# Softmax maxima of an attention kernel folded through DRAM, and its SP transfers issued a few to a turn

## The chip, the cores and the metric

The kernel runs on one core of a Trainium2 chip. The metric is device time in microseconds, the median of 3 runs: 1323.48 us before the change (1323.15 to 1324.08). In the text, PE is the matrix engine, ACT the scalar engine (activations), DVE the vector engine, POOL the general engine, and SP the engine that here only issues transfers.

## What is computed

One transformer block in float32 on x of shape (4, 1024, 256): attention with 16 heads of 16, then a gated feed-forward block of width 1024. Both are "sandwiched": layer norm goes in, layer norm comes out, and the result is added to x.

```python
def stable_softmax(x):
    x_max = jnp.max(x, axis=-1, keepdims=True)
    exp_x = jnp.exp(jnp.clip(x - x_max, -50.0, 50.0))
    return exp_x / (jnp.sum(exp_x, axis=-1, keepdims=True) + 1e-6)
...
scores = einsum('bhqd,bhkd->bhqk', q, k) * scale
out = einsum('bhqk,bhkd->bhqd', stable_softmax(scores), v)
...
x = x + layernorm(attention(layernorm(x)))
x = x + layernorm(ffn(layernorm(x)))   # silu(w1)*w2, gelu(h1), gelu(h2), w3
```

The kernel takes the exponential of the scores without subtracting their maximum. The small 1e-6 beside the sum then has to be multiplied by the largest exponential of the row: denominator = 1e-6 * max + sum. The kernel keeps that maximum only for the first 128 queries of each half of a sequence; it is what the change is about.

## The kernel before

**Attention, in tiles.** A *tile* is one (batch b, group g of 4 heads, half h of 512 queries, chunk c of 128 keys, pair u of heads): 4 x 4 x 2 x 8 x 2 = 512 tiles, in this order. For each, `exponentials` (L444) lets PE make scores `s` of 128 keys x 2 heads x 512 queries into one of three two-bank slots of PSUM (pool `ps`, tag `big`), and ACT writes their exponentials `e` into a ring of four pairs of tiles. `weigh` (L454) multiplies a pair of tiles by the values `vaug` into the one-bank accumulator `acc`; a column of ones in `vaug` gives the sum beside the 16 outputs of each head, so each head has a slot of 32 rows of which 17 are used. `rise` (L461) folds a pair into the running maximum `top` on DVE, 128 keys x 4 heads x 128 queries.

**Units.** 16 tiles with one (b, g, h) are a *unit*; there are 32, and two units (both halves) are a group's work. At its end `unit_end` (L632) copies `acc` to `o` on DVE and adds the division (`divide`, L470) to the side work: PE transposes the four heads of `top` (L478) and the four blocks of `o` (L480) into a slot of tag `big`, DVE reduces the transposed maxima to `em` (L482), makes denominators and their reciprocals, and writes the quotients to `on` (L488). After a batch's last group the `ending` follows: transposes of `on`, output projection, norm, residual.

**Turns and side work.** The main loop (L937) works in *turns*: three tiles of scores and exponentials, the maxima and weighted sums of earlier tiles, then one call of `side.take` (L582). Everything else (projections for the next batch, flags, endings, divisions, copies of weights to a rounded form) consists of `Step`s in chains. A turn takes at most one step with PE work; a step is due `gap` turns after the one before it in its chain. In a *calm* turn, close to a unit's end, only PE steps are taken. Steps marked heavy are not taken in two turns running. PE steps other than divisions use the one-bank space `misc`, the *side bank*. A division sets `side.borrowed`, and the next turn then makes one tile fewer before its weighted sums.

**Transfers.** The order in which each engine gets its instructions is the order of the program. SP issues, among others, the *stacks*: for a group, q and k, split into high and low parts, are copied from `cq`/`ck` into 64-row layouts `sq`/`sk` by 32 transfers of 64 KB (`copies` L404, `stack` L419). There are two sets of stacks, so the copies for group g + 2 are issued when group g has ended (L661), and wait for its last scores. At the start, `load_rest` (L198) issues the loads of the output weights, x of batches 2 and 3, and scales behind the first stack. Late in the last batch, the feed-forward's weights are loaded into space that q, k and the stacks leave free (L652, L665).

**Feed-forward.** After the last unit, PE multiplies for 8 halves of sequences through the four layers (`gated`, `gelu_layer`, `finish`); side work there is norms and checks of the weights.

Of the kernel before, what the change touches and what calls it, by code (L numbers as in the profile page):

```python
# [18 lines left out]
P = 128  # L19
HEADS = 16  # L20
DH = 16
# [3 lines left out]
PARTS = 4  # L25
ROWS = PARTS * DH
RING = 8
TURN = 3
LN_EPS = 1e-5
SM_EPS = 1e-6  # L30
# [40 lines left out]
class Step:  # L71


    def __init__(self, run, gap=0, tensor=True, heavy=False):
        self.run, self.gap, self.tensor, self.heavy = run, gap, tensor, heavy
        self.ready, self.patient = lambda: True, heavy


# [37 lines left out]
def tile_fast(ctx: ExitStack, tc: tile.TileContext, x, wqk, wv, wo, w1, w1s, w2, w2s, h1, h1s, h2, h2s, w3, w3s, out, bad):  # L116
# [11 lines left out]
    xpool = ctx.enter_context(tc.tile_pool(name="x", bufs=1))  # L128
    small = ctx.enter_context(tc.tile_pool(name="small", bufs=3))
    dram = ctx.enter_context(tc.tile_pool(name="rounded", bufs=1, space=bass.MemoryType.DRAM))  # L130


    xs = [xpool.tile([P, NT, D], F32, tag=f"x{b}", name=f"x{b}") for b in range(B)]
# [8 lines left out]
    def load_x(b, halves=range(NH)):  # L142
        view = x[b].rearrange("(t p) d -> p t d", p=P)
        for h in halves:
            for at, tokens in pieces(h, view):
                nc.sync.dma_start(out=xs[b][:, at, :], in_=tokens)
# [31 lines left out]
    with ExitStack() as actx, ExitStack() as rctx:  # L178
# [11 lines left out]
                    load_x(0, [1])  # L190
        nc.scalar.dma_start(out=wv_sb, in_=wv.rearrange("(c p) d -> p c d", p=P))

        def load_wo(c):
            for h in range(HPT):
                r = SLOT * (HPT * c + h)
                nc.sync.dma_start(out=wo_sb[DH * h : DH * (h + 1), c, :], in_=wo[r : r + DH, :])

        def load_rest():  # L198

            for c in range(DC):  # L200
                load_wo(c)
            for b in range(2, B):
                load_x(b)
            for name, w in (("w1", w1s), ("w2", w2s), ("h1", h1s), ("h2", h2s)):
                nc.sync.dma_start(out=scales[name], in_=w)
            nc.sync.dma_start(out=w3s_sb, in_=w3s.partition_broadcast(P))


        cq = {(w, m, k): keep.tile([P, S], F32R, name=f"c{'qk'[w]}{m}{k}") for w in range(2) for m in range(DC) for k in ("hi", "lo")}
# [25 lines left out]
        def misc(name):  # L235
            return ps_misc.tile([P, NQ], F32, tag="misc", name=name)
# [30 lines left out]
        def prologue(b, space, copy):  # L267
# [60 lines left out]

            def squares(w, m, h):
                def run():  # L330
                    sq = st["sq", w, m] = work.tile([P, NQ], BF16, tag="sq", name="sq", bufs=4)
                    hi = cq[w, m, "hi"][:, h * NQ : (h + 1) * NQ].bitcast(F32)
                    nc.scalar.activation(sq, hi, AF.Square)

                return run
# [68 lines left out]
        def copies(g, w, c0=0, c1=S):  # L404
# [11 lines left out]

            return [copy(u, j, n) for u in range(2) for j in range(PARTS) for n in range(2)]

        def stack(b, g):  # L419
            for w in (1, 0):  # L420
                for copy in copies(g, w):
                    copy(nc.sync)
            stacked[g % 2] = b, g

        def slots(b, g, t0=0, t1=NT):

# [7 lines left out]
            return run  # L434


        stacked, slotted = [None] * 2, [None] * 2
        tiles = [(b, g, h, c, u) for b in range(B) for g in range(NG) for h in range(NH) for c in range(NT) for u in range(2)]

        def pair(k):  # L440
# [20 lines left out]
        def rise(k):  # L461
# [4 lines left out]
            if c:  # L466
                top = tops[b, g, h]
                nc.vector.tensor_max(top, top if c > 1 else pair(k - 2)[:, :, :, 0:P], pair(k)[:, :, :, 0:P])  # L468

        def divide(g, h, o, top):  # L470


            def run():
                side.borrowed = True
                both = ps.tile([P, 2, NQ], F32, tag="big", name="po")
                po, pm = both[:, 0], both[:, 1].rearrange("p (i k) -> p i k", k=P)
                for i in range(HPG):
                    nc.tensor.transpose(pm[:, i], top[:, i // 2, i % 2], ident)  # L478
                for t in range(TPQ):
                    nc.tensor.transpose(po[:, t * P : (t + 1) * P], o[:, t * P : (t + 1) * P], ident)  # L480
                em = small.tile([P, HPG], F32, tag="em", name="em")
                nc.vector.tensor_reduce(em, pm, AX.X, ALU.max)  # L482
                po = po.rearrange("p (t i s) -> p t i s", t=TPQ, s=SLOT)
                den = small.tile([P, TPQ, HPG], F32, tag="den", name="den")
                nc.vector.scalar_tensor_tensor(den[:, 0], em, SM_EPS, po[:, 0, :, DH], ALU.mult, ALU.add)
                nc.vector.tensor_copy(den[:, 1:], po[:, 1:, :, DH])
                nc.vector.reciprocal(den, den)
                nc.vector.tensor_mul(  # L488
                    on[h][:, :, HPG * DH * g : HPG * DH * (g + 1)].rearrange("p t (i e) -> p t i e", e=DH),
                    po[:, :, :, 0:DH], den.unsqueeze(3).to_broadcast([P, TPQ, HPG, DH]),  # L490
                )

            return [Step(run, 1)]

# [56 lines left out]
        class Side:  # L551


            def __init__(self):
                self.first, self.rest, self.slot = [], [], 0
                self.tired = False
                self.borrowed = False

            def add(self, steps, first=False):
                chain = [list(steps), self.slot]  # L560
# [21 lines left out]
            def take(self, calm=False):  # L582

                self.slot += 1
                self.borrowed = False
                free, heavy = True, False
                for chain in self.first + self.rest:
                    while (step := self.due(chain, self.slot, free)) and (step.tensor or not calm):
                        chain[0].pop(0)
                        chain[1] = self.slot  # L590
                        step.run()
                        free = free and not step.tensor
                        heavy = heavy or step.heavy
                self.tired = heavy
# [5 lines left out]
        side = Side()  # L600
        accs, tops, ends, later = {}, {}, {}, {"qk1": None}

        def begin(b):

            if b + 1 < B:
                norm, xt, qk, v, flags = prologue(b + 1, misc, to_vector)

                def first_made():
                    later["qk"] = b + 1
                    side.add(flags[0])  # L610

                def second_made():
                    later["qk1"] = b + 1
                    side.add(flags[1])


                steps = norm[0] + norm[1] + xt[0]
                for i, step in enumerate(qk[0][0]):
                    steps += [step, xt[1][i]]
                steps += xt[1][TPQ // 2 :] + qk[0][1]  # L620

                xt[0][TPQ // 2].ready = lambda: later["qk1"] == later["v"] == b
                v = v + [Step(lambda: later.update(v=b + 1), 0, False)]
                qk1 = sum(qk[1], [])
                for step in qk1:
                    step.gap, step.patient = 2, False
                qk1 = qk1 + [Step(second_made, 0, False)]
                later["rest"] = [Step(lambda: side.add([Step(lambda: None, 5, False)] + qk1), 0, False)] + v

                later["chain"] = side.add([Step(lambda: None, 0 if b else 4, False)] + steps + [Step(first_made, 0, False)])  # L630

        def unit_end(b, g, h):  # L632
# [2 lines left out]
            to_vector(o, accs[b, g, h])  # L635

            assert g or not b or not any(step.tensor for step in ends[b - 1, h][0])
            unit = side.add(divide(g, h, o, tops[b, g, h]), True)
            if g == NG - 1:
                last = ending(b, h, to_scalar if (b, h) == (B - 1, NH - 1) else to_vector)  # L640
                for step in last:
# [7 lines left out]
            if n >= NG:  # L649
                n, at = n - NG, b + 1  # L650
            if b == B - 1 and g == NG - 2:
                load_weights("h1", range(HC // 2))  # L652
            if at < B:
                put = Step(slots(at, n), 0, False)
                if at > b:
                    assert later["qk"] == at
                    later["chain"][0].append(put)
                else:
                    assert later["qk1"] == at
                    put.run()  # L660
                stack(at, n)  # L661
            if g == NG - 3 and b + 1 < B:
                later["chain"][0].extend(later["rest"])
            elif g == NG - 3:
                side.add([Step(lambda n=n: load_weights(n), 1, False) for n in ("w1", "w2", "w3")])  # L665
                side.add([Step(lambda: None, 7, False)] + prepare(0, to_vector))
            if g == NG - 1:
                begin(b + 1)
# [38 lines left out]
        def prepare(n, copy):  # L707
# [24 lines left out]

                return run

            return norm_steps(rows, st) + [Step(apply(i), 1, False) for i in range(0, TPQ, 2)] + [Step(transposes(c), 1) for c in range(DC)]

        def product(p, n, m, i, c):
            for k, half in enumerate(i):
# [180 lines left out]
        v[0].run()  # L919
        alone = False  # L920
        load_x(1)
        stack(0, 1)
        load_rest()
        early = [v[1], Step(slots(0, 0, 0, NT // 2), 0, False)]
        side.add(early + v[2:] + [Step(slots(0, 0), 0, False), Step(slots(0, 1), 0, False)] + sum(qk[1], []) + [Step(lambda: later.update(qk1=0, v=0), 0, False), Step(lambda: side.add(flags[0] + flags[1]), 0, False)])
        begin(0)
        side.add([s for k in blocks for s in round_weights(*k)])
        made = seen = weighed = 0

# [7 lines left out]
        while weighed < len(tiles):  # L937
            n = end = made
            end += TURN
            make(end - side.borrowed)  # L940
            if made == len(tiles):
                n = made
            for k in range(seen, n - 1, 2):
# [260 lines left out]
```

## Time and profile before

| what | value |
|---|---|
| median of 3 runs | 1323.48 us |
| profiled execution: device time, span | 1322.63 us, 1320.8 us |
| granted PE clock | 0.995 |
| busy share of the span: PE, DVE, ACT, POOL | 96%, 53%, 55%, 9% |
| exponentials, 512 of 128 x 1024 | 485.1 us busy, 1034 ns each |
| running maxima of 128 x 512, 192 later ones of a unit | 134.6 us busy, 701 ns each |
| stack copies, 64 KB each, SP | 2.3 us from issue to landing (median) |
| weight loads of 512 KB, POOL | 5.5 us to landing (median) |

The page's strip of 40 slices shows two halves. In the first 20 slices ACT is 70 to 80% busy and the DMA engines 30 to 80%; from slice 21 on ACT falls to 10 to 40% and PE's weight loads rise from 30 to 80%: that is the feed-forward. A busy share averages over both, so each half is read by itself. Rows of matrix work overlap, and their ends are modelled: how far apart their *starts* are tells more of PE than their durations.

### The profile page before, as it was taken

How to read it: one execution, taken by the hardware profiler on the slowest of the kernel's cores; microseconds unless marked ns; L12 is line 12 of the kernel's file. 1: busy time of each engine (PE TensorE's matmuls, PEld its weight loads, DVE VectorE, ACT ScalarE, POOL GpSimd, SP SyncE). 2: the span in 40 equal slices, each digit the busy share in tenths (PEclk: the TensorE clock that was granted, in tenths of full speed). 3: DMA queues.
4: the chain of work that ended last, by engine and by line, in shares of the span. 5: the costliest groups of instructions: out<-in, count | busy, mean ns of one | idle time of the engine just before them, and what ended most of it. 6: DMA issues, size and time to landing. Idle time of an engine off the chain costs nothing.

```text
span 1320.8 us, 21125 instructions
## 1 busy us (share of the span) xinstructions
PE 1267.2 (96%) x8194; PEld 777.2 (59%) x8194; DVE 696.2 (53%) x1518; ACT 724.1 (55%) x902; POOL 119.1 (9%) x166
## 2 busy tenths in 40 slices
PE   7999999999999999988999999999999999999995
PEld 3333333333333333333578888788887888878885
DVE  3456457654685445645662634736446364463533
ACT  4788887888888888898631412314223142231410
POOL 6212112121120000000000000000000000000000
PEclk9999999999999999999999999999999999999998
DMA  4685543466443333343220000201101011020000
GB/s 131 171 212 131 118 114 94 110 143 152 73 114 61 50 50 65 65 95 129 80 113 1 24 1 1 64 25 32 56 1 64 24 33 57 1 64 8 17 0 19
DMA packets 45518, 91.30 MB, mean 69 GB/s; under 512 B 12000, under 2 KB 22880, under 8 KB 45408
## 3 DMA queue, kind: packets, MB, share of 16 engines
q1 hardware_dynamic: 37520, 65.20, 21.4%
q0 software_dynamic: 7360, 24.12, 5.8%
q8 instruction: 67, 1.10, 0.4%
q10 hardware_dynamic: 528, 0.52, 0.1%
q14 instruction: 43, 0.35, 0.1%
HBM read 40.52 MB, written 15.73 MB: 43 GB/s over the span
## 4 chain that ended last, share of the span: by engine, by line
PE 76%; DVE 10%; ACT 9%; issue 3%; POOL 1%; DMA 1%; SPq 0%; ACTq 0%; POOLq 0%; DVEq 0%
PE ph L739 35%; PE acc L459 12%; PE s L451 8%; ACT e L452 7%; PE pg L739 5%; PE pz L792 4%; PE p L259 4%; PE py L259 2%; PE pv L259 2%; DVE top L468 2%; PE po L480 1%; DVE sg L755 1%; DVE o L265 1%; DVE st L94 1%; DVE ha_lo L744 1%
## 5 line engine op out<-in xcount | busy, mean ns | idle before, releaser
L452 ACT ACTIVATE e<-s 128x1024 f32<-128x1024 f32 x512 | 485.1, 1034 | 54.5 <-PE s L451 42.9
L459 PE MATMUL acc<-e,vaug 128*32 128x512 f32 x2048 | 255.1, 600 | 2.6 <-POOL vaug L429 2.6
L775 ACT ACTIVATE a<-ph,h_scale 128x512 f32<-128x512 f32 x128 | 81.1, 686 | 306.6 <-PE ph L739 306.6
L451 PE MATMUL s<-sq,sk 64*128 64x512 f32 x1024 | 193.2, 449 | 17.6 <-ACT e L452 15.0
L739 PE MATMUL ph<-hb_hi,h 128*128 128x512 f32 x512 | 199.5, 390 | 0.0
L739 PE MATMUL ph<-hb_lo,h 128*128 128x512 f32 x512 | 199.4, 389 | 0.0
L451 PEld LDWEIGHTS s<-sq,sk 64*128 64x128 f32 x1024 | 86.2, 184 | 158.3 <-ACT e L452 125.8
L468 DVE TENSOR_TENSOR top<-top,e 128x512 f32<-128x512 f32 x192 | 134.6, 701 | 42.0 <-ACT e L452 35.4
L459 PEld LDWEIGHTS acc<-e,vaug 128*32 128x32 f32 x2048 | 49.2, 108 | 107.2 <-issue 97.6
L104 POOL TENSOR_TENSOR rstd<-ve,minus_half 128x4 f32<-128x4 f32 (+1 forms) x33 | 37.5, 1137 | 803.1 <-DVE ve L102 803.1
L739 PEld LDWEIGHTS ph<-hb_hi,h 128*128 128x128 f32 x512 | 96.1, 188 | 20.2
L739 PEld LDWEIGHTS ph<-hb_lo,h 128*128 128x128 f32 x512 | 96.1, 188 | 20.1
L776 DVE CAST ha_hi<-a 128x512 fp32r<-128x512 f32 x64 | 27.1, 424 | 142.5 <-ACT a L775 142.5
L739 PE MATMUL ph<-ha_hi,sq 128*128 128x512 f32 x256 | 101.8, 398 | 0.3
L739 PE MATMUL ph<-ha_lo,sq 128*128 128x512 f32 x256 | 99.9, 390 | 0.0
L739 PE MATMUL ph<-ha_lo,sk 128*128 128x512 f32 x256 | 99.7, 390 | 0.0
L739 PE MATMUL ph<-ha_hi,sk 128*128 128x512 f32 x256 | 99.7, 390 | 0.0
L753 ACT ACTIVATE sg<-pg,w_scale 128x512 f32<-128x512 f32 x64 | 43.3, 688 | 55.0 <-DVE ha_lo L744 43.1
L755 DVE SCALAR_TENSOR_TENSOR sg<-pg,w_scale,sg 128x512 f32<-128x512 f32 x64 | 47.1, 745 | 48.0 <-ACT sg L753 48.0
L776 DVE CAST hb_hi<-a 128x512 fp32r<-128x512 f32 x64 | 27.0, 422 | 71.3 <-ACT a L775 71.3
L259 PE MATMUL p<-xT,wqk_sb 128*32 128x512 f32 x512 | 61.1, 598 | 1.5 <-ACT xT L262 0.9
L739 PEld LDWEIGHTS ph<-ha_hi,sq 128*128 128x128 f32 x256 | 48.4, 189 | 12.7 <-DVE sg L755 3.3
(158 smaller groups left out, 1648.2 us busy)
## 6 DMA issues: line engine op xcount, KB each, us to landing
w<-in_h_dram POOLq DMA_DIRECT2D x16, 512.0 KB, 5.5
h_r<-wr POOLq DMA_DIRECT2D x16, 512.0 KB, 3.8
x<-in_h_dram SPq DMA_DIRECT2D x32, 256.0 KB, 2.7
sk<-ck1hi SPq DMA_DIRECT2D x64, 64.0 KB, 2.3
sk<-ck1lo SPq DMA_DIRECT2D x64, 64.0 KB, 2.3
sq<-cq1hi SPq DMA_DIRECT2D x64, 64.0 KB, 2.3
sq<-cq1lo SPq DMA_DIRECT2D x64, 64.0 KB, 2.3
h<-h_r SPq DMA_DIRECT2D x8, 512.0 KB, 6.5
```

Source lines behind the costliest of these rows:

```text
L104: nc.gpsimd.tensor_tensor(rstd[:, :n], ve[:, :n], self.minus_half[:, :n], ALU.pow)
L259: nc.tensor.matmul(o[j : j + SLOT, :], w[:, j : j + SLOT], i, **flags)
L451: nc.tensor.matmul(s[:, a, :], stacks[1, g % 2, u][r, c * P : (c + 1) * P], stacks[0, g % 2, u][r, h * NQ : (h + 1) * NQ], start=True, sto ...
L452: nc.scalar.activation(pair(k)[:, u], s, AF.Exp)
L459: nc.tensor.matmul(acc[SLOT * i : SLOT * (i + 1), :], vaug[g % 2][:, c, i, :], pair(k)[:, i // 2, i % 2, :], start=c == 0, stop=c == NT - 1)
L468: nc.vector.tensor_max(top, top if c > 1 else pair(k - 2)[:, :, :, 0:P], pair(k)[:, :, :, 0:P])
L739: nc.tensor.matmul(p, homes[n][c][:, m * P : (m + 1) * P], half[:, c, :], start=c == 0 and k == 0, stop=c == len(homes[n]) - 1 and k == 1)
L753: nc.scalar.activation(sg, p[:, 0, :], AF.Silu, scale=scales["w1"][:, m : m + 1])
L755: nc.vector.scalar_tensor_tensor(sg, p[:, 1, :], scales["w2"][:, m : m + 1], sg, ALU.mult, ALU.mult)
L775: nc.scalar.activation(a, p[:, j, :], AF.Gelu, scale=scales[n][:, m : m + 1])
L776: nc.vector.tensor_copy(o[0][:, m, :], a)
L792: nc.tensor.matmul(p[t], half[:, c, t * P : (t + 1) * P], homes["w3"][c], start=c == 0 and k == 0, stop=c == HC - 1 and k == 1)
```

## The change

The maxima of a unit no longer go through four transposes. `top` (128 keys x 4 heads x 128 queries) is written to DRAM at the unit's end and read back with head and key sharing the partitions: 32 partitions for a head, each with 4 keys of 128 queries. Two maxima on DVE fold the 4 keys to one, and one transpose then suffices for all four heads. Its 128 columns go into the parts of the 32-column slots in `po` which the transposed outputs leave unused (columns 20 to 27 of each), so the whole division fits into the side bank. It consists of three steps: `back` (in the turn of the unit's end), `fold` (two turns later), `run` (one more). The two units of the last batch's last group keep the old form (`divide_last`). `side.borrowed` is gone.

The transfers of stacks are taken five to a turn, other loads four to a turn or one in two turns, as `quiet` steps, which calm turns take too. A stack counts as outstanding until its steps are done, and the first projection into the space that it reads waits for that. The flags of both halves of the projections form one chain, and `sq` has two buffers instead of four.

```diff
@@ constants, Step
+HOLE = 20
...
-    def __init__(self, run, gap=0, tensor=True, heavy=False):
-        self.run, self.gap, self.tensor, self.heavy = run, gap, tensor, heavy
+    def __init__(self, run, gap=0, tensor=True, heavy=False, quiet=False):
+        self.run, self.gap, self.tensor, self.heavy, self.quiet = run, gap, tensor, heavy, quiet
...
+    shuffle = ctx.enter_context(tc.tile_pool(name="shuffle", bufs=2, space=bass.MemoryType.DRAM))
@@ load_rest returns a list, x of batch 2 first
+            rest = [load_half(2, h) for h in range(NH)]
...
@@ squares
-                    sq = st["sq", w, m] = work.tile([P, NQ], BF16, tag="sq", name="sq", bufs=4)
+                    sq = st["sq", w, m] = work.tile([P, NQ], BF16, tag="sq", name="sq", bufs=2)
@@ stack
+        def few(run_all, n=5):
+            def some(part):
+                return lambda: [run() for run in part]
+            return [Step(some(run_all[i : i + n]), 1, False, quiet=True) for i in range(0, len(run_all), n)]
+
         def stack(b, g):
-            for w in (1, 0):
-                for copy in copies(g, w):
-                    copy(nc.sync)
-            stacked[g % 2] = b, g
+            outstanding.append((b, g))
+
+            def done():
+                stacked[g % 2] = b, g
+                outstanding.remove((b, g))
+
+            steps = few([lambda copy=copy: copy(nc.sync) for w in (1, 0) for copy in copies(g, w)])
+            steps[0].ready = lambda: g < GPT or later["qk1"] == b
+            return steps + [Step(done, 0, False, quiet=True)]
@@ divide
+            there = shuffle.tile([HPG, P, P], F32, tag="top", name="top_d")
+            folded = work.tile([P, P // SLOT, P], F32, tag="folded", name="folded", bufs=1)
+            nc.sync.dma_start(out=there.rearrange("i k q -> k i q"), in_=top.rearrange("p u n q -> p (u n) q"))
+
+            def back():
+                nc.sync.dma_start(out=folded, in_=there.rearrange("i (k s) q -> (i k) s q", s=P // SLOT))
+
+            def fold():
+                for n in (2, 1):
+                    nc.vector.tensor_max(folded[:, 0:n], folded[:, 0:n], folded[:, n : 2 * n])
+
             def run():
-                side.borrowed = True
+                p = misc("po")
+                for t in range(TPQ):
+                    nc.tensor.transpose(p[:, t * P : (t + 1) * P], o[:, t * P : (t + 1) * P], ident)
+
+                pm = p.rearrange("p (n s) -> p n s", s=SLOT)[:, :, HOLE : HOLE + P // (TPQ * HPG)]
+                nc.tensor.matmul(pm, folded[:, 0], ident.rearrange("p (n k) -> p n k", n=TPQ * HPG), start=True, stop=True, is_transpose=True)
+                em = small.tile([P, HPG], F32, tag="em", name="em")
+                nc.vector.tensor_reduce(em, pm.rearrange("p (i n) k -> p i n k", i=HPG), AX.XY, ALU.max)
+                po = p.rearrange("p (t i s) -> p t i s", t=TPQ, s=SLOT)
+                quotients(g, h, em, po)
+
+            return [Step(back, 1, False, quiet=True), Step(fold, 2, False), Step(run, 1)]
@@ Side.take
-                    while (step := self.due(chain, self.slot, free)) and (step.tensor or not calm):
+                    while (step := self.due(chain, self.slot, free)) and (step.tensor or step.quiet or not calm):
@@ begin
+                for m in range(DC):
+                    qk[m][0][0].ready = lambda m=m: not any(at == b and g // GPT == m for at, g in outstanding)
@@ unit_end
-            unit = side.add(divide(g, h, o, tops[b, g, h]), True)
+            unit = side.add((divide_last if (b, g) == (B - 1, NG - 1) else divide)(g, h, o, tops[b, g, h]), True)
...
-                load_weights("h1", range(HC // 2))
+                side.add([Step(lambda c=c: load_weights("h1", [c]), 2 if c else 0, False, quiet=True) for c in range(HC // 2)])
...
-                stack(at, n)
+                side.add(stack(at, n))
...
-                side.add([Step(lambda n=n: load_weights(n), 1, False) for n in ("w1", "w2", "w3")])
+                chunks = [(n, [c]) for n in ("w1", "w2") for c in range(DC)] + [("w3", range(c, c + 4)) for c in range(0, HC, 4)]
+                side.add([Step(lambda n=n, c=c: load_weights(n, c), 2, False, quiet=True) for n, c in chunks])
@@ start of attention
-        stack(0, 1)
-        load_rest()
...
+        side.add(stack(0, 1) + few(load_rest(), 4))
...
-            make(end - side.borrowed)
+            make(end)
```

`quotients` holds the lines of the old division from `den` on, unchanged.

## The prediction

> **What bounds the kernel now.** I read the span and clock first (1320.8 us at 0.995, so no disturbance to correct for), then the windows, then the waits, then the timeline around one division. The last row of exponentials ends at 641.45 us and the feed-forward starts at 642.48: from there on PE is busy for 99.9% of each 100 us window, on matmuls that the change does not touch. I cost that half (679 us) at nothing; what can move lies in attention, 53.7 us (first division) to 641 us.
>
> ```profile
> core 0: us, PE busy (x) PEld busy (x) DVE busy (x) ACT busy (x) POOL busy (x), PEclk, DMA share, GB/s
> 50.00:640.00 590.00, 559.59 (x4608) 209.45 (x4604) 332.64 (x697) 507.37 (x577) 75.12 (x97) 1.00 0.46 102
> ...
> ACT e L452 <- PE s L451: 42.3, 54, 1.7
> ACT e L452 <- DVE top L468: 6.8, 8, 1.1
> ```
>
> The windows row shows two engines near their limit: PE 95% by records whose ends are modelled, ACT 86%. DVE (56%), POOL and the DMA engines (46%) have room. ACT's waits (both rows are of the same window) say what its idle time is: 42.3 us of exponentials waiting for scores, 6.8 us waiting for DVE to free a pair of the ring. ACT stays full only as long as PE delivers scores in time, and three score slots (2.7 us of ACT, at a median distance of 906 ns between exponentials) are all the reserve.
>
> Around the division at the end of unit (2, 3, 1), the timeline of all engines:
>
> ```profile
> 462.81 1.06 PE L459 MATMUL acc<-e,vaug 128*32 128x512 f32 x8
> 463.80 0.66 PE L478 MATMUL po<-ident,top 128*128 128x128 f32 x4
> 464.69 0.66 PE L480 MATMUL po<-ident,o 128*128 128x128 f32 x4 [0.23 <-DVE o L265]
> 465.27 0.73 PE L451 MATMUL s<-sq,sk 64*128 64x512 f32 x4
> ...
> 465.87 2.86 ACT L452 ACTIVATE e<-s 128x1024 f32<-128x1024 f32 x3 [0.81 <-PE s L451]
> ...
> 466.67 0.42 DVE L488 TENSOR_TENSOR on<-po,den 128x256 f32<-128x256 f32 x1
> ...
> 466.95 0.50 PE L451 MATMUL s<-sq,sk 64*128 64x512 f32 x2
> ```
>
> PE goes from the weighted sums to eight transposes, has to wait among them for the copy of the accumulator (o), and issues scores again 1.47 us after the first transpose; ACT has run dry by 0.81 us. The division holds one of the three score slots from 463.80 until the last DVE row ends at 467.09, 3.29 us. I followed ACT's rows from division to division: of the first 30, 26 are followed within 2.2 us by such a hole, **23.5 us in sum** (from 0.18 to 1.65 us each), and up to 5 us later come another **8.4 us** of holes before exponentials, where the third slot is missing or DVE is late.
>
> **The change, part by part.**
>
> *Divisions off the score slots, and later.* 30 of the 32 divisions take the new form; the last unit pair (3, 3) keeps the old one. The step at the unit's end now issues no PE work, so the 1.47 us go from that place: PE runs from the sums to the scores. A turn is 3 of 512 tiles in the 614.5 us from first to last exponential, 3.6 us. Three turns later PE does five transposes in the side bank, where `o` and the folded maxima are long there. Price of those: rows of one shape start 109 ns apart, and from the first of four to the next scores it is 0.59 us, so 0.15 us is the change of shape; five make 0.55 + 0.15 = 0.70 us. Net for PE 1.47 - 0.70 = 0.77 us, times 30: **23 us**. For ACT: 23.5 + 8.4 = **32 us** of holes lose their cause, less what the new place costs. That is little: between its score batches such a turn puts 1.5 pairs of sums (0.86 us each, from 16 rows in 1.85 us) and 0.70 us, 2.0 us, under the 2.7 us of reserve. I take the lower of the two sums, for PE then becomes the next to be late: the heavy steps (projections, 1.86 us) already cause the other holes, some 50 of ACT's 87 us idle between 30 and 642 us, and nothing of them goes. Lower end 12 us (only the three transposes saved, 30 x 3 x 0.109 = 10, plus part of the 5.2 us that PE waits for `o`), upper end 32 plus a few of the 6.8.
>
> *Fifth transpose into holes.* It writes 16 runs of 8 numbers, 32 apart. No row here has a matmul with a broken output; the nearest is the transpose of the same shape, 109 ns. [...] By the row the five cost 0.55 us[...]. I take the row[...].
>
> *DVE.* Added: two maxima, 128x256 and 128x128. From 702 ns at 512 wide and 425 at 256 (another pair of operands): 0.43 + 0.29 us. Removed: the 128x512 reduction (690 ns) becomes 128x128, about 0.28. Net +0.31 us, 9 us over 30, hidden on an engine with 44% idle; the chain of 1.7 us that stands in one piece behind `o` falls into two, which helps the 6.8 us. If DVE's cover were gone it would cost those 9 us. `fold` waits in DVE's queue for the transfer back; behind it stand the maxima (ring slots, so ACT) and copies out of the side bank (so PE). Out: 256 KB in 512-byte rows; nearest the 384 KB stores in 1 KB rows, 2.8 us. Back: 256 KB in 2 KB rows; nearest the checks' loads of 256 KB, 2.7 us. Under load I allow 6.0 and 5.5 us (x's 384 KB loads; the 512 KB loads of POOL's queue). So 5.5 to 11.5 us from unit end; `fold` is due two turns after it, 7 to 9 us (484.3 to the second next side step at 491.4; 463.8 to 473.05). I take no wait; by the loaded ends it is up to 4 us, of which the ring of eight tiles absorbs most.
>
> *Queue of SP.* Each issue takes 0.61 us (rows of four copies: 2.44 to 2.49). 32 copies for a group are 20 us. New in a group: two times out, its landing, and back, about 1.2 + 3 us each, 8.5 us in which SP stands still with the copies behind. 28 of 38 us; landed 30 us after the group's end, against first use at some 34 (the group's last scores are at 459.9, 4 us before its end). Cost nothing, with about 4 us to spare, against 22 before. Spreading itself doesn't pace SP, which runs ahead of PE; it sets who stands behind whom. Spreading the first loads, and FFN weights in pieces, moves transfers with tens of us to spare: nothing either way. The gate on projections replaces waits that cost ACT 0.8 us. Flags in one chain, `sq` with two buffers and one turn more before the feed-forward's first transposes: off the path, each within a few turns of slack; nothing.
>
> **Sum.** Own time of the profiled execution 1322.63 us (span 1320.8 and 1.8 around it). 1322.63 - 23 = 1299.6; the median shown is 0.85 higher, 1323.48, so 1300.4. Of the 9 us between PE's and ACT's sums I add a tenth for the freed slot: **1299.5 us**.
>
> **Rivals.**
> - *The hole moves along (gain 3 to 15 us, about 1314).* PE at 95% is the real bound; what is saved at the unit's end is eaten by heavy steps that now fall into the free turn, and only the transposes and `o` waits are won: 10 us. For: 50 us of ACT's holes belong to no division. Against: PE's 95% contains modelled ends, and 15 us of waits for ACT stand before score rows.
> - *The round trip is the bound (slower, about 1335).* SP holds its queue during each trip. From the point where the trips and copies of a group last more than 4 us longer than I reckon, the group's first scores wait for their copies, and each further us is paid at 14 group starts; 1.7 us more undo the 23 us, 2.5 us more give 1323.5 - 23 + 35 = 1335. For: 64 KB copies, x and POOL's 512 KB loads share the engines (46% busy, 79% at 66 to 100 us). Against: copies land 2.3 us after issue even so.
> - *It does not do what it says*: `fold` held on DVE keeps the side bank occupied, and PE waits for it in the next turn. Half the gain, 1311; it lies within the first rival's range.
> - *More than the sum*: both ACT sums and part of the other holes, over 33 us, 1288.
>
> **Numbers.** The sum as reckoned, 1289 to 1308: 0.58. Hole moves along or side bank held, 1308 to 1320: 0.22. Over 33 us: 0.07. No difference: 0.03. Round trip as the bound: 0.10. The range 1285 to 1317 leaves the slower case, no difference, and the ends out. Faster by over 0.2% (2.6 us, about what this measurement can tell from no change): 0.86; within: 0.04; slower: 0.10.
>
> **What would show it.** Right: no L478-like top transposes inside attention but at its end; ACT's wait for scores falls from 42 to below 25 us, nearly all of that within 5 us of unit ends; attention ends near 618 us, the feed-forward takes the same 679 us; the five transposes stand at 109 ns. Wrong: the fifth transpose longer; `fold` with idle time released by the transfer back; score rows released by a DMA at group starts; ACT's sum of holes unchanged while they sit after heavy steps.

## The result, and the profile after

The changed kernel takes 1311.05 us (median of 4 runs, 1305.83 to 1312.02) against 1323.52 before: a ratio of 0.9897, interval 0.9871 to 0.9924. That is 12.5 us, about half of the 24 forecast. It lies inside the range, but in the branch from 1308 to 1320 to which the prediction gave 0.22. Its runs spread over 6 us where those of before spread over 1. The profiled execution took 1312.02 us (span 1310.2).

Every line number below is the changed kernel's own unless "before" is said; L470, L471 and L478 are now scores, exponentials and weighted sums, L505 and L508 the trip's two transfers, L512 the fold, L517 and L520 a division's transposes.

Where did the time go? Read from the last exponential in the timeline: attention ends at 634.4 us instead of 641.4 (7 us; from its first exponential it takes 606.3 us instead of 614.6), and the rest takes 675.8 us instead of 679.4 (3.6 us). Neither half is as forecast. First ACT's waits, from 50 to 640 us of the changed kernel (sum in us, times, longest):

```profile
ACT e L471 <- PE s L470: 24.7, 35, 2.5
ACT e L471 <- issue: 11.3, 3, 7.5
...
ACT e L471 <- DVE top L487: 3.6, 5, 0.8
```

The 42.3 us of waits for scores have become 24.7, as forecast. The holes at unit ends are gone: counted from the last row of a unit's sums, over the first 30 units, ACT's holes before exponentials were 22.6 us within 2.3 us and 6.7 us in the next 2.8 us; now 2.9 and 2.0. But there is a new row, "issue": three holes of 11.3 us in sum for which no releaser of ACT's is found, one of 7.55 us. The waits of all engines in the same window say where they come from:

```profile
DVE folded L512 <- DMA folded<-top_d: 41.3, 15, 7.7
...
PEld po L520 <- DVE folded L512: 13.6, 6, 8.0
...
PE po L520 <- DVE folded L512: 12.0, 4, 7.8
```

The fold on DVE waited for the transfer back in 15 of 30 divisions, and behind it PE waited four times with the fifth transpose (PEld is the weight load of the same transposes, so the last two rows are not to be added up). The longest case, in the timeline of all engines (start, length, engine, instruction, idle time before it):

```profile
98.45 2.43 SPq L418 DMA_DIRECT2D sq<-cq1hi  x4
100.94 2.49 SPq L418 DMA_DIRECT2D sq<-cq1lo  x4
...
101.96 0.66 PE L517 MATMUL po<-ident,o 128*128 128x128 f32 x4
103.48 0.58 SPq L418 DMA_DIRECT2D sq<-cq1hi  x1
104.16 0.53 SPq L505 DMA_DIRECT2D top_d<-top  x1
106.73 0.33 SPq L508 DMA_DIRECT2D folded<-top_d  x1
...
109.60 0.75 DVE L512 TENSOR_TENSOR folded<-folded 128x256 f32<-128x256 f32 x2 [7.67 <-DMA folded<-top_d]
...
110.40 0.47 PE L520 MATMUL po<-ident,folded 128*128 128x128 f32 x1 [7.79 <-DVE folded L512]
110.81 1.65 PE L470 MATMUL s<-sq,sk 64*128 64x512 f32 x6
...
111.69 2.85 ACT L471 ACTIVATE e<-s 128x1024 f32<-128x1024 f32 x3 [7.55 <-issue]
```

The unit had ended at 92.4 us, but SP issued its way out only at 104.16: from 92.24 on it issued 17 copies of the next stack and one other load, the last of them shown here. PE had already begun the division's transposes at 101.96 and then stood in the middle of them for 7.8 us. Every later score row is behind it in PE's order. I worked out the same for all trips, from the issue and landing times of the rows of L505, L508 and L512 (us from the end of the unit's sums; units are counted from 0 in this table, from 1 in the text):

```
unit (half)      out issued   out landed   back landed   fold's idle time
4  (first)          1.3          4.7          10.1           5.33
5  (second)        -2.5         -0.2           2.6           0
12 (first)          3.4          5.9          11.4           5.29
13 (second)        -2.5          0.2           3.1           0
28 (first)          3.8          6.3           9.3           5.12
29 (second)        -0.4          4.2           7.0           0
```

It is the units of the first half that are late: 13 of the 15 waits are theirs. At a group's end (second half) SP is free, and the trip is issued at once. Half a group later the group's copies stand ahead of it. How full the queue is shows at its other end. In groups 1 to 14 (the first group is 0) the last copy of a stack lands only 0.7 to 3.9 us before the group's first scores, where before it was 6 to 21 us. In the last group it comes too late, and the scores wait 2.8 us for it (at 598.5 us).

### The profile page after: what moved, and what is told of

It reads as the page before. It is cut to its first block, busy times and chain, and to the rows that moved or that the text cites. A ratio compares the mean times of both kernels' runs of the same rounds, so it can differ in the third digit from the quotient of the medians.

```text
span 1310.2 us, 21118 instructions
## 1 busy us (share of the span) xinstructions
PE 1247.4 (95%) x8104; PEld 770.6 (59%) x8104; DVE 701.3 (54%) x1578; ACT 723.2 (55%) x902; POOL 118.0 (9%) x166
## 4 chain that ended last, share of the span: by engine, by line
PE 68%; DVE 10%; DMA 7%; ACT 6%; SPq 5%; issue 2%; ACTq 0%; POOL 0%; POOLq 0%; DVEq 0%
PE ph L796 36%; PE acc L478 10%; PE s L470 7%; SPq L418 5%; PE pz L849 4%; ACT e L471 4%; PE pg L796 3%; PE p L264 3%; DMA folded<-top_d 3%; PE py L264 2%; DVE sg L812 2%; DMA top_d<-top 2%; DVE ha_lo L801 1%; PE pv L264 1%; DVE st L95 1%
## 5 line engine op out<-in xcount | busy, mean ns | idle before, releaser
L471 ACT ACTIVATE e<-s 128x1024 f32<-128x1024 f32 x512 | 483.9, 1036 | 45.7 <-PE s L470 26.2
L478 PE MATMUL acc<-e,vaug 128*32 128x512 f32 x2048 | 257.4, 605 | 0.9 <-POOL vaug L448 0.7
L470 PE MATMUL s<-sq,sk 64*128 64x512 f32 x1024 | 186.0, 446 | 18.7 <-ACT e L471 12.6
L470 PEld LDWEIGHTS s<-sq,sk 64*128 64x128 f32 x1024 | 86.2, 186 | 137.1 <-ACT e L471 108.5
L487 DVE TENSOR_TENSOR top<-top,e 128x512 f32<-128x512 f32 x192 | 135.3, 705 | 18.3 <-ACT e L471 12.2
L478 PEld LDWEIGHTS acc<-e,vaug 128*32 128x32 f32 x2048 | 49.5, 109 | 108.3 <-issue 104.1
L833 DVE CAST ha_hi<-a 128x512 fp32r<-128x512 f32 x64 | 27.1, 424 | 141.8 <-ACT a L832 141.8
L796 PE MATMUL ph<-ha_lo,sq 128*128 128x512 f32 x256 | 99.9, 390 | 0.0
```

Source lines behind the costliest of these rows:

```text
L470: nc.tensor.matmul(s[:, a, :], stacks[1, g % 2, u][r, c * P : (c + 1) * P], stacks[0, g % 2, u][r, h * NQ : (h + 1) * NQ], start=True, sto ...
L471: nc.scalar.activation(pair(k)[:, u], s, AF.Exp)
L478: nc.tensor.matmul(acc[SLOT * i : SLOT * (i + 1), :], vaug[g % 2][:, c, i, :], pair(k)[:, i // 2, i % 2, :], start=c == 0, stop=c == NT - 1)
L796: nc.tensor.matmul(p, homes[n][c][:, m * P : (m + 1) * P], half[:, c, :], start=c == 0 and k == 0, stop=c == len(homes[n]) - 1 and k == 1)
L833: nc.vector.tensor_copy(o[0][:, m, :], a)
```

## The experiments

All times are medians of 4 runs, compared with the kernel before on the same chip, which took 1323.2 to 1324.0 in every set. The last two columns are of the one profiled execution, which can lie up to 3.5 us beside the median (e11).

| kernel | us | ratio to before, interval | last exponential ends | from there to the end |
|---|---|---|---|---|
| before | 1323.5 | | 641.4 | 679.4 |
| changed | 1311.05 | 0.9897 (0.9871 to 0.9924) | 634.4 | 675.8 |
| e1 no trip | 1286.22 | 0.9716 (0.9699 to 0.9732) | 609.7 | 675.4 |
| e2 trip unread | 1300.09 | 0.9824 (0.9800 to 0.9849) | 620.5 | 675.6 |
| e3 spread only | 1318.13 | 0.9957 (0.9940 to 0.9974) | 640.1 | 675.3 |
| e4 gap back to one | 1314.13 | 0.9933 (0.9912 to 0.9954) | 631.4 | 679.6 |
| e5 four a turn | 1303.96 | 0.9851 (0.9834 to 0.9868) | 625.2 | 675.5 |
| e6 fold later | 1306.47 | 0.9872 (0.9845 to 0.9899) | 631.1 | 675.5 |
| e7 loads behind | 1309.33 | 0.9898 (0.9881 to 0.9914) | 629.5 | 675.8 |
| e8 both of these | 1303.22 | 0.9846 (0.9830 to 0.9862) | 627.5 | 675.5 |
| e9 trip on POOL | 1294.21 | 0.9780 (0.9763 to 0.9797) | 619.9 | 673.4 |
| e10 POOL, gap, weights | 1289.58 | 0.9737 (0.9721 to 0.9754) | 615.1 | 673.5 |
| e11 back on POOL | 1305.00 | 0.9851 (0.9834 to 0.9868) | 628.9 | 677.7 |
| e12 POOL, in a burst | 1290.04 | 0.9746 (0.9730 to 0.9763) | 614.8 | 673.4 |

**What the parts are worth: e1 to e4.** My first theory was that the trip comes late; the rival was that the hole at a unit's end has only moved to the heavy steps.

e1 takes the trip away and leaves the division where it is. In e1 and e2 the denominators are without the term 1e-6 times the maximum:

```diff
-            nc.sync.dma_start(out=there..., in_=top...)
             def back():
-                nc.sync.dma_start(out=folded, in_=there...)
+                pass
             def fold():
-                ...
+                pass
@@ run: four transposes of o, no fifth, no em
-                nc.vector.scalar_tensor_tensor(den[:, 0], em, SM_EPS, po[:, 0, :, DH], ALU.mult, ALU.add)
-                nc.vector.tensor_copy(den[:, 1:], po[:, 1:, :, DH])
+                nc.vector.tensor_copy(den[:, t0:], po[:, t0:, :, DH])   # t0 = 0
```

> The divisions of the changed kernel stay where they are, but without the trip through DRAM, the two folds, the fifth transpose and the maximum (the term 1e-6 times the maximum is left out of the denominator). Theory A, late trip: DVE's waits for the folded maxima (41.3 us in 15 places) are what the gain is missing, since PE and then ACT stand behind them; 1311 falls to 1296 to 1301, near the forecast. Theory B, hole moves along: the free turns have been filled by heavy steps and the trip costs next to nothing; only the 30 fifth transposes go (about 3 us), 1306 to 1310.

1286.22 us, 10 better than even the first theory expected. The division out of the score slots is worth far more than forecast, and the trip, with its folds and the fifth transpose, takes 25 us of it back.

e2 puts the two transfers back, and nothing reads what they bring:

> As the run before, but both transfers of the trip are issued as in the changed kernel and nobody reads what comes back (the maximum is left out again). It tells the wait from the traffic. Theory A says the wait alone costs: same as without the trip within 2 us. If SP's standing still for the landing, or the traffic, delays copies that scores need, it lies clearly above, up to the changed kernel's 1311. Theory B: equal to the run before as well, but both at 1306 to 1310.

1300.09, clearly above e1: it is not the wait alone. The trip costs 14 us without being read, and reading it (waits, folds, fifth transpose) another 11. Unit lengths, taken from every sixteenth exponential, show that the 14 us are not spread out. e1 and e2 agree within 0.1 us in all units except two: the fifth lasts 27.1 us instead of 17.5, the thirty-first 20.8 instead of 16.8. PE's timeline of e2 at the first of them:

```profile
102.51 0.73 PE L470 MATMUL s<-sq,sk 64*128 64x512 f32 x4
110.02 1.49 PE L470 MATMUL s<-sq,sk 64*128 64x512 f32 x2 [6.78 <-DMA sq<-cq1lo]
111.44 1.93 PE L478 MATMUL acc<-e,vaug 128*32 128x512 f32 x8
```

Scores wait 6.78 us for a copy of their own stack. SP's timeline of e2 just before (L507 and L510 are the trip here):

```profile
100.84 0.58 SPq L418 DMA_DIRECT2D sq<-cq1hi  x1
101.51 0.54 SPq L507 DMA_DIRECT2D top_d<-top  x1
104.05 0.33 SPq L510 DMA_DIRECT2D folded<-top_d  x1
104.48 1.78 SPq L418 DMA_DIRECT2D sq<-cq1hi  x3
106.31 2.48 SPq L418 DMA_DIRECT2D sq<-cq1lo  x4
```

The trip stands among the copies; SP waits from 102.05 to 104.05 for the way out to land, and the last seven copies follow. This was the slower rival of the prediction, here at two groups instead of fourteen. Over the whole run SP's own waits hold this row (e2, same columns as above):

```profile
SPq L510 <- DMA top_d<-top: 66.3, 30, 4.7
```

e3 has all of the change but the new division (old division in the score slots, with `borrowed`):

> The spread transfers and everything else of the change, with the old division in the score slots. Theory A: the spreading gives nothing in attention (SP runs ahead of PE anyway); what is left is the feed-forward's later transposes, 3 to 4 us: 1319 to 1321. If the spreading itself costs, because copies for a group land late, it is above 1323; if it gives, below 1317.

1318.13, a little below the expected span. Attention ends 1.3 us earlier, of which 0.9 is an earlier start; the other 4 us are behind it, in the feed-forward. From e3 to e1 the time falls by 31.9 us. That step does not only move the division: its four transposes of `top` go as well, and the turn with one tile fewer. These parts were not tried apart.

e4 undoes one number:

```diff
-[Step(transposes(c), 1 if c else 2) for c in range(DC)]
+[Step(transposes(c), 1) for c in range(DC)]
```

> The changed kernel with the gap before the feed-forward's first transposes back at one turn. The stretch from the last exponential to the end is 679.4 us before and 675.8 after, though no matmul of it was changed. If the gap of two turns is why, that stretch returns to about 679 and the time rises by 3 to 4 us, to 1314 or 1315; if the loads in pieces or an earlier start are why, it stays near 676.

The stretch returns to 679.6 us, as before, and the time rises by 3 us. So it is the gap. The rows of these transposes between 690 and 1200 us, before and then after (count, busy time, mean ns):

```profile
L728 PE MATMUL fpt<-ident,fxn 128*128 128x128 f32 x48 | 10.2, 292 | 0.0
```

```profile
L785 PE MATMUL fpt<-ident,fxn 128*128 128x128 f32 x48 | 7.2, 272 | 0.0
```

In some halves before, at 841.94 us for one, the first four transposes took 1.21 us instead of 0.60: their weight loads waited one by one for `fxn` from DVE. The waits of all engines in the same stretch hold that row before, and none for `fxn` after:

```profile
PEld fpt L728 <- DVE fxn L112: 1.9, 10, 0.2
```

These 3.0 us are most of the 3.6. Waits of 0.2 us between the four of a group are hard to see in a busy share of 99.9%; the busy and mean time of the row show them.

**Waits, or order: e5 to e8.** The second question was what repairs it on SP's queue.

e6, the fold one turn later (`Step(fold, 3, False)`):

> The changed kernel with the fold three turns after the unit's end instead of two. Without the trip the kernel takes 1286 us, with a trip that nobody reads 1300, with the trip read 1311. Theory A1: those last 11 us are DVE's and PE's waits for the folded maxima; one turn (3.6 us) more takes 41 us of waits to some 10, and the time to 1300 to 1304. Theory B1: they are the two folds on DVE and the fifth transpose (30 times 0.4 and 0.1 us on busy engines), which a later fold leaves as they are: 1309 to 1312.

1306.47: between the two. The waits for the fold shrank from 41.3 us in 15 places only to 32.2 in 9, with one of 12.2 us; that one held PE (12.08 us of idle ACT), and in another way than in the changed kernel:

```profile
112.36 0.75 DVE L512 TENSOR_TENSOR folded<-folded 128x256 f32<-128x256 f32 x2 [12.22 <-DMA folded<-top_d]
113.03 0.68 DVE L270 TENSOR_SCALAR xT<-pt 128x512 f32<-128x512 f32 x1
113.77 1.11 PE L517 MATMUL po<-ident,o 128*128 128x128 f32 x4 [10.24 <-DVE xT L270]
```

PE stands before the division's first transpose. The division needs the side bank, and the copy that empties it (`xT`) is behind the fold in DVE's order. That is the prediction's third rival. Where the trip is late by a whole group's copies, one turn does not cover it, and where it was late by 2 us, it does.

e7, the first loads one a turn instead of four, and the feed-forward's weights nine turns later:

```diff
-        side.add(stack(0, 1) + few(load_rest(), 4))
+        side.add(stack(0, 1) + few(load_rest(), 1))
...
-                side.add([Step(lambda n=n, c=c: load_weights(n, c), 2, False, quiet=True) for n, c in chunks])
+                side.add([Step(lambda: None, 9, False, quiet=True)] + [Step(lambda n=n, c=c: load_weights(n, c), 1, False, quiet=True) for n, c in chunks])
```

> The changed kernel, with the first loads (x, output weights, scales) one a turn instead of four, and the feed-forward's weights begun nine turns later, behind the last stack. Theory A2: the 14 us that the unread trip costs are two places where a group's copies land late, at 105 us and at 580 us, because SP has there to issue these loads, 32 copies and two trips in one group's time; here both go, and with them part of the folds' waits: 1311 falls to 1295 to 1302. Theory B2: the 14 us are traffic (256 KB twice in each unit), spread over all groups: 1309 to 1312.

1309.33, a miss for theory A2. It lies in theory B2's span, but traffic spread over all groups does not fit e2's unit lengths, nor e9 below. The two late stacks are cured (the thirty-first unit 16.8 us again), but the first loads now stand among the copies two groups later: a fold waits 11.56 us at 146 us. PE again waits for the side bank (7.15 us, for a reader that stands behind the fold), and ACT 8.26.

e8, both edits:

> Both edits at once: loads behind the stacks, and the fold a turn later. Theories A1 and A2 together: 1288 to 1293, the time without a trip and a few us for folds and the fifth transposes. If the two repair the same us, it is no better than the better of them alone.

1303.22, ten over the upper end of what was expected. The unit ends at 127.4 us and its way out is issued 11.2 us later. In attention's first 150 us, SP with the trip has more to issue than fits, in both orders tried.

e5, four copies to a turn instead of five (`few(run_all, n=4)`). In this run the load of the second gate's weights overtakes the last copies of q in the last batch's last group, so these scores are of overwritten data, and only its times are of use:

> The changed kernel with four copies of a stack to a turn instead of five. Theory C, SP's queue is full: a group asks of SP 20 us of issues, two trips with their standing still, and in places other loads, in 37 us; five or four only changes what stands ahead of a trip. Fewer copies ahead of the first half's trip (5 or 6, 3 us) take away part of the folds' waits of 41 us, and a stack that ends a turn later gives it back where copies are late: 1306 to 1312. Theory D, only the order ahead of the trips is wrong: the folds' waits go, 1300 or less.

1303.96, between the two, and the folds' waits 13.2 us in 5 places. In steady state the order ahead of the trips was the fault (theory D): of the units from the sixth on, only three folds wait at all, for 2.2 us at most. What is left are the same two places, 26.6 and 21.3 us long.

**Another queue: e9 to e12.** e9 issues both transfers from POOL (`nc.gpsimd.dma_start`):

> The changed kernel with both transfers of the trip issued by POOL instead of SP. Theory A: SP no longer stands still for the landings (66 us in 30 places) and nothing stands ahead of the trip but POOL's own weight loads, in the first 380 us; copies land as without the trip: 1290 to 1298, with the folds' waits gone after 400 us. If traffic is what costs: 1305 or more. Against it: POOL's waits for its 512 KB loads (up to 7 us) now stand ahead of the trip, and the trip's ahead of the copies of values.

1294.21, as the theory had it: the same traffic, 17 us less (2 of them at the program's very end, see the last section). The copies land in time again, mostly 10 to 17 us before a group's first scores. But the folds still wait 21.4 us in 12 places, and six of these are after 400 us, where the theory had none. The way out is now issued at most 1.3 us after a unit's end; from there to landing back a trip takes 6.1 to 10.5 us (5.0 to 8.7 from SP's queue), and some folds are due earlier.

e10 adds the later fold and the weights behind the last stack:

> The trip on POOL's queue (1294 us) with the fold a turn later and the feed-forward's weights behind the last stack. With the trip on POOL, 21 us of waits for the fold were left in 12 places of up to 3.8 us, and the last unit was 3.8 us longer than without a trip. If a fold's wait is what the rest costs, one turn takes nearly all of it: 1287 to 1291, the time without a trip plus the fifth transposes (3 us). If the turn later only shifts the fold behind other work, 1293 to 1296.

1289.58. Its waits, of all engines from 50 to 640 us:

```profile
POOL folded L508 <- DMA top_d<-top: 49.2, 18, 4.7
...
DVE folded L512 <- DMA folded<-top_d: 2.3, 2, 1.9
```

It is now POOL that stands still for the landing, and PE's weight loads wait only 0.6 us for POOL in all attention; the folds wait 2.3 us in all. This beats both kernels: 21 us better than the changed kernel, 34 than before. It is 3.4 us from e1. That 30 fifth transposes of 109 ns are 3.3 is chance: from first to last exponential e10 takes 6.1 us more than e1 (586.8 and 580.6), and some 2 us less at the program's end.

e11 sends the way out by SP and the way back by POOL:

> Out on SP, back on POOL. The number of issues on SP falls by 30 of 0.33 us only (10 us in all attention, none of it on a path), but SP no longer stands still until the way out has landed (66 us). Theory C, standing still: about the time of the whole trip on POOL, 1293 to 1298. If it is the way out behind the copies, and not the standing still, that costs: 1304 to 1311.

1305.00. After 130 us it runs as e9 does (the units of batch 1 to 3 agree but for a few tenths in most). The loss lies before: SP issues the way out of the first unit 5.2 us and of the third 7.7 us after their ends, behind first loads and copies. So standing still is not the fault by itself. But e11 also loses 4.4 us against e9 behind the last matmul, in a closing instruction of POOL (last section). With that instruction at 6.3 us in all three, the changed kernel, e11 and e9 would be at 1311.1, 1302.6 and 1296.2 (an estimate from the medians and one trace of each): the way back and the standing still are worth some 8 us, the way out some 6. The copies' margin agrees: 4 to 10 us before a group's first scores in e11, but for the last group's 0.7.

e12 is e10 with all 32 copies of a stack in one turn again:

> The best version so far (trip on POOL, fold a turn later, weights behind: 1289.6 us) with the 32 copies of a stack issued in one turn again. If spreading helps only because trips stand in the same queue, it is worth nothing once they are elsewhere: 1288 to 1292. If bursts of copies by themselves disturb (traffic beside the trip, or copies standing ahead of the first x loads), 1293 or more.

1290.04: no difference from e10. With the trip on POOL the spreading serves nothing, and bursts disturb nothing.

## Why the prediction came out as it did

The range and the direction held, but by luck, through errors of opposite sign: 1318.1 (spread only) minus 32 (division off the score slots) plus 14 (trip in SP's queue) plus 11 (trip awaited) gives 1311. The prediction had -23 for the division and nothing for the rest.

- *"I take the lower of the two sums, for PE then becomes the next to be late"* was wrong: 31.9 us came from e3 to e1, and with the whole division in place 28.5 from e3 to e10 (2 of them at the program's end). That this is so near ACT's sum is partly chance. ACT's holes before exponentials shrink from 54.4 us in e3 to 23.4 in e1. Of these 31 us, 24 stood within 6 us of a unit's last sums (28.3, then 4.7); 8 stood 8 to 12 us behind it (14.3, then 6.0), among the holes of which the prediction said that nothing goes. That PE can run on with scores into three free slots would explain both, but was not tried apart. That the hole would only move along (the first rival) is refuted by e1.
- The five transposes at 0.70 us: right. In the changed kernel 382 to 386 ns from the first to the fourth, 109 to the fifth, 202 or 203 to the next scores, 0.69 us; in e1 the 202 follow the fourth directly. So the fifth costs **109 ns** with its output in 16 runs of 8 numbers, as much as the row with an unbroken output (109 ns) from which the prediction priced it.
- *"I take no wait; by the loaded ends it is up to 4 us, of which the ring of eight tiles absorbs most"* is the step that failed most. The trip's durations were well guessed (2.5 and 3.2 us median against 2.8 and 2.7); the time that it stood before being issued, up to 11.6 us, was left out. And DVE comes to the fold not 7 to 9 us after a unit's end but 3.3 to 9.9, in 14 of 30 divisions before 7. 41.3 us of waits, up to 7.67, and no ring helps, for PE itself waits, between two transposes.
- *"which runs ahead of PE" (of SP), "about 4 us to spare", loads with "tens of us to spare"*: the first is true only between trips. The way out waits for the unit's last maximum (107.9 us of SP's waits), so everything behind it in the queue is tied to the unit's end. The 4 us themselves were well reckoned (0.7 to 3.9 in the changed kernel), and gone in two groups of e2, where other loads shared the queue.
- Transfers spread: nothing by themselves (0.4 us in attention from its first exponential in e3, none in e12), as costed.
- *One turn more before the feed-forward's first transposes: nothing* was wrong, 3 to 4 us of gain. I read the busy share and did not look at how long single rows took.
- *"`fold` held on DVE keeps the side bank occupied"* (the third rival, which named 1311) is a part, not the main cause. In the changed kernel PE waited for quotients (DVE on L495) 3.1 us in all, and twice, for 1.7 and 0.6 us, for a reader of the side bank behind a waiting fold. The four waits in the midst of the transposes are 12.0 us. In e6 and e7 the longest wait was of the rival's kind (10.24 and 7.15 us). That its figure was hit is luck.
- A slip without effect: the division shown in the prediction ends unit (2, 2, 1), not (2, 3, 1).

What stays open: how much of the last 11 us (e2 to the changed kernel) are the folds' 0.7 us on DVE; e10 says at most 6, since all that is done there and its attention is 6.1 us longer than e1's. Why the changed kernel's runs spread over 6 us was not tried apart.

## What to carry to other kernels

This round trip through memory was hidden by the time from its issue, not from its place in the program: look for what stands ahead of it in the issuing engine's queue (here up to 11.6 us), and for what is behind while that engine waits for the first leg to land (on SP 66.3 us in 30 waits). A queue with slack was cheaper here (1294.21 us in e9) than a better order in a full one (1303.22 in e8). And where an instruction waited for data in the midst of a group of PE work (7.79 us, with 7.55 of idle ACT behind it), or in front of the copy that empties a space that PE needs next (10.24 us in e6, with 12.08 of idle ACT), buffers on other engines did not help, so price such a wait at full length.

## What the hardware showed unasked

A long wait of PE cost more than itself. The windows of the changed kernel around the 7.8 us wait (length, busy time by engine, granted clock, DMA share, GB/s):

```profile
92.00:100.00 8.00, 8.00 (x66) 2.40 (x58) 3.21 (x6) 7.49 (x10) 1.81 (x2) 1.00 0.75 181
100.00:116.00 16.00, 7.79 (x40) 2.49 (x39) 5.75 (x14) 6.70 (x8) 0.00 (x0) 0.68 0.48 96
116.00:124.00 8.00, 7.67 (x58) 3.04 (x58) 3.37 (x6) 6.33 (x8) 1.30 (x2) 1.00 0.18 41
```

The granted clock falls to 0.68 over the window with the wait: it is 0.50 from 107 to 112 us, and 1.00 again from 116 to 118. PE is slow just when it resumes: 16 rows of sums take 3.56 us there (from 112.38) instead of the usual 1.92 seen at other places of the same timeline, and ACT has a second hole of 2.55 us at 117.09. Shorter waits were not always free either: PE's timeline of the changed kernel has one at 559 us, and the window behind it (same columns as above) is at half clock:

```profile
556.58 0.66 PE L517 MATMUL po<-ident,o 128*128 128x128 f32 x4
559.44 0.47 PE L520 MATMUL po<-ident,folded 128*128 128x128 f32 x1 [2.20 <-DVE folded L512]
```

```profile
559.50:562.90 3.40, 3.40 (x15) 1.34 (x19) 3.09 (x9) 2.18 (x3) 0.00 (x0) 0.50 0.29 48
```

At half clock for 3.40 us, that is some 1.7 us lost besides the 2.2 (an estimate). Most waits of this size left the clock alone: of the seven between 1.2 and 2.8 us in this trace's attention, this is the only one with such a stretch behind it. The longest of them, 2.77 us at 598.5 us, has none, so what brings the clock down is not shown here. Over the run the mean is 0.987 against 0.995 before, and 0.995 again in e10; but the first 50 us, ahead of the first division, already differ (0.90 against 0.97), so the waits are only a part of that.

The last step of the program differs too. Behind the last matmul, POOL has a closing instruction, named DRAIN in the trace. It takes 6.27 us in each of the ten traces in which POOL issues 76 transfers, before and changed kernel among them. In e9, e10 and e12, with 136, it takes 4.31 us, and in e11, with 106, 8.72. The stretch from the last exponential to the last matmul does not differ between these (662.0 to 662.6 us, all but before and e4), so this is the whole of what the table shows there: some 2 us less with the trip on POOL, 2 more in e11. Why the drain varies so was not tried.
